# State sums by transposes, a gate by token and two value products in a fused sequence kernel

## The chip, the cores and the metric

The kernel runs on one core of a Trainium2 chip. The metric is the device time of one execution in microseconds (us). The engines are PE (TensorE: products and transposes; PEld is its weight load), DVE (VectorE), ACT (ScalarE), POOL (GpSimd) and SP (which issues most DMAs). Each works through its own queue in order.

## What is computed

Eight sequences of 256 tokens with 128 channels go through four double layers; everything is in float32, and after each part there is a residual sum and a layer norm. Two parts matter here. One is the local attention block (run twice, in two layers): 8 heads of 64, windows of 64 tokens, each token looks at its own window and the one before.

```python
bk, bv = (look_around(bk), look_around(bv))   # the window before, and the own one
sim = einsum('bhwid,bhwjd->bhwij', bq, bk)
mask = (i < j) | (i > j + WINDOW) | (j == -1)
attn = softmax(where(mask, -max, sim))
out = einsum('bhwij,bhwjd->bhwid', attn, bv)
```

The other is the Mamba block that follows, with 256 inner channels and 16 states:

```python
x_inner, z = split(x @ W_in)
xc = silu(conv(x_inner) + conv_b)
delta = softplus(delta_raw * w_dt + b_dt)      # delta_raw, B, C = xc @ W_xproj
h = exp(delta * A) * h + delta * B * xc        # a scan over the tokens, 16 states
y = sum over states of (h * C)
y = y + xc * D_param
return (y * silu(z)) @ W_out
```

The rest (a gated recurrence before; two mixtures of experts, two attention pairs and typed attention after) is not edited.

## The kernel before

The program is written in six stages: `rglru`, `local_mamba`, `moe1`, `chunked`, `moe2`, `typed`. In `local_mamba` the activations lie with the 128 channels on the partitions and the tokens along them. `one_sequence` (inside `local_mamba`, L1335) runs two local blocks and a norm for one sequence; four sequences are live at a time, and as each ends, `mamba_sequence` (L1223) for it is started beside the next ones (`interleave`, L256, called at L1470).

That is only the order in which instructions are recorded. `_Order` (L312) then sets the order on each engine: `plan` (L612) is a list scheduler with a cost table (`LENGTHS`, L352: how long each form keeps its engine, and when its result is there), a bias added to the priority of each engine, tile and stage (`BIAS`, L328), and a reluctance to change ACT's function table or the shape of PE's tiles (`STAY`, L327). The order that it finds is imposed on every engine's queue. It knows Exp and Ln as one group of functions.

The parts that the change touches:

- Values of the local block (L1124 to L1128). The attention of a 128-token half works on 64-token windows, so the values are needed for tokens 0 to 127, 64 to 191 and 128 to 255. For each of these three shifts one product `vps` of 128x512 is made on PE and copied from PSUM by ACT into `v[:, a, :]`. In the second half of the sequence the scores (L1142) take the keys `k[r, g, k0 : k0 + P]` with k0 = 64 for the queries 128 to 191, under the mask `band` that the tables hold (L148).
- The gate (L1246 to L1252): z with its channels on the partitions, Silu by ACT into `sz`. Two Silu and a load of the combined exponential and logarithm table (`exp_ln`, L898) follow each other there.
- Scan and state sums (L1293 to L1310). For each of 8 pairs of states: four exponentials `da` on ACT (L1302), and on DVE the product `hs` (L1304), the scan (L1306) and the product with C (L1307), each over 128x1024. Then PE adds the two states of the pair into one PSUM bank, `yp`, by a product with the identity matrix (L1309): two products of 128x512 per pair, 128 in the whole kernel. A float32 product is two instructions in the profile, so there are 256.
- The end (L1311 to L1317): DVE adds the skip term xc * D to the sum (L1313, two instructions per sequence, read from PSUM), POOL (DVE for the last sequence) multiplies with the gate (L1314), and the result goes as moving operand into the output projection `wout`.

L870 is the one line in `mm` that issues every product, so the profile tells these by their tiles.

Of the kernel before, what the change touches and what calls it, by code (L numbers as in the profile page):

```python
# [81 lines left out]
def _tables():  # L82
# [65 lines left out]
    madd("band", np.concatenate([mask((i < k0) | (i > k0 + 64)), mask((k0 < w) | (k0 > w + 64))], 1))  # L148
# [163 lines left out]
class _Order:  # L312
# [14 lines left out]
    STAY = dict(PE=80, ACT=740)  # L327
    BIAS = {  # L328
        "ACT  1": 100, "ACT  5": 585, "ACT bt 3": 5, "ACT bt 5": -775, "ACT d 2": -425, "ACT da 2": -45, "ACT e 2": -5, "ACT e 4": 965, "ACT e 6": -20,
        "ACT got 3": 575, "ACT h 2": -200, "ACT ix 4": 15, "ACT k 2": 265, "ACT lavp 2": 210, "ACT lnrs 1": -10, "ACT lnrs 2": -160, "ACT lnsq 1": -135,  # L330
        "ACT lnsq 2": 15, "ACT ot 2": 10, "ACT ptsb 2": -595, "ACT ptsb 6": -515, "ACT q 2": 20, "ACT qsq 2": 10, "ACT r 2": -5, "ACT rg 1": 10,
        "ACT rg 2": -915, "ACT rn 2": 15, "ACT rs 4": 340, "ACT rs 6": -690, "ACT s 6": 200, "ACT sakq 2": -10, "ACT sg 3": -550, "ACT sh 5": -2525,
        "ACT spe 1": -220, "ACT spt 1": -50, "ACT st 6": 100, "ACT sz 2": 280, "ACT v 2": 885, "ACT vs 4": 320, "ACT xchunked 2": 15, "ACT xs 2": -610,
        "DVE biasfull 3": -335, "DVE biaspart 3": -20, "DVE bt 5": -5, "DVE c 1": 590, "DVE centre 0": 320, "DVE d 2": 10, "DVE decaypart 4": -600,
        "DVE e 4": 570, "DVE four 4": 100, "DVE fs 4": -70, "DVE gate 4": 340, "DVE get 2": 200, "DVE got 4": 530, "DVE identb 0": -50, "DVE k 6": 500,
        "DVE lg 2": 2240, "DVE lo 4": -265, "DVE mv 4": -660, "DVE mv 5": 100, "DVE mv 6": -485, "DVE nm 2": -3975, "DVE nm 6": 4960, "DVE nth 4": -45,
        "DVE oh 2": -725, "DVE oh 5": -10, "DVE ptsb 2": -3895, "DVE ptsb 6": 895, "DVE put 4": -395, "DVE put 5": 55, "DVE q 5": -825, "DVE q 6": -475,
        "DVE rc 2": -1225, "DVE rc 6": 10, "DVE route 2": -55, "DVE s 5": 10, "DVE sares 2": 70, "DVE sel 2": -1590, "DVE sg 3": -140, "DVE sm 4": 2720,
        "DVE spl 1": -215, "DVE ss 2": 370, "DVE st 4": 85, "DVE st 6": 1645, "DVE sum 4": 170, "DVE t 2": 440, "DVE u 2": 250, "DVE vs 4": 50,
        "DVE we 4": 1425, "DVE xc 2": 460, "DVE xla 4": -15, "DVE xlocal 2": -5, "DVE xmoe 5": -200, "DVE xmoe 6": -580, "DVE xpf 4": -370,  # L340
        "DVE xrglru 2": 120, "DVE xsa 4": 80, "DVE z 4": -1990, "PE a 2": -100, "PE acc 5": 155, "PE b 2": -35, "PE bt 3": 75, "PE bt 5": 50,
        "PE cum 2": -995, "PE cum 4": -25, "PE cum 5": -615, "PE fold 2": 2915, "PE g 2": -4155, "PE gate 2": 785, "PE kps 4": 135, "PE less 2": 295,
        "PE lg 2": 1680, "PE lg 4": 50, "PE ln 2": -10, "PE o 2": 10, "PE o 6": -10, "PE pg 5": 150, "PE ps 4": -15, "PE pt 4": -130, "PE pu 3": 220,
        "PE py 3": -200, "PE py 5": 170, "PE qk 2": 25, "PE qkt 2": -720, "PE raw 2": -8675, "PE rows 2": 400, "PE sc 2": -50, "PE sc 4": 65, "PE sc 6": 5,
        "PE v 5": 290, "PE vps 2": 4075, "PE vps 4": 25, "PE wo 2": 75, "PE wo 6": -85, "PE wout 2": -115, "PE xin 2": 1180, "PE xps 2": -2540, "PE y 2": 20,
        "PE z 2": -450, "PE zt 5": 560, "PE zt 6": 25, "POOL d 2": 130, "POOL e 6": -30, "POOL got 4": -200, "POOL h 2": 370, "POOL k 5": 400,
        "POOL k 6": 850, "POOL km 6": 1240, "POOL mean 0": 1510, "POOL places 5": -200, "POOL q 6": 20, "POOL rest 4": -65, "POOL rg 1": -800,
        "POOL rg 2": -200, "POOL rot 2": -400, "POOL s 6": -750, "POOL t 2": 550, "POOL zero 0": -655, "POOL zeros 1": 385, "SP bc 2": -970, "SP cst 3": 5,
        "SP got 3": 355, "SP got 5": 350, "SP rottable 0": 80, "SP rows 4": 210, "SP rowschunked 4": -105, "SP vec 0": -830, "SP w 0": 15, "SP w 3": 115,
        "SP wattn 2": 585, "SP wffn 2": 705, "SP wlocal 0": 1175, "SP wmoe 4": 520, "SP xs 2": -105, "SP ybuf 5": -200,  # L350
    }
    LENGTHS = {  # L352
        "ACT  LoadActFuncSet  ": (1178, 1283), "ACT d Ln 128x512 128x512": (535, 640), "ACT da Exp 128x255 128x255": (398, 503),
        "ACT e Abs 128x256 128x256": (460, 565), "ACT e Exp 128x128 128x128": (420, 525), "ACT e Exp 128x256 128x256": (461, 566),
        "ACT e Exp 128x512 128x512": (527, 632), "ACT four Exp 128x2 128x2": (100, 205), "ACT got DMACopy 128x512 128x512": (454, 3611),
        "ACT h TensorCopy 64x255 64x255": (295, 400), "ACT lnrs Exp 128x256 128x256": (315, 420), "ACT ot TensorCopy 128x512 128x512": (486, 591),
        "ACT qsq Square 128x512 128x512": (494, 599), "ACT r Relu 128x256 128x256": (460, 565), "ACT rg Exp 128x1020 128x1020": (1039, 1144),
        "ACT rg Exp 128x1024 128x1024": (998, 1103), "ACT rg Ln 128x1024 128x1024": (950, 1055), "ACT rn Exp 128x16 128x16": (110, 215),
        "ACT rn Ln 128x16 128x16": (112, 217), "ACT rs Exp 128x2 128x2": (96, 201), "ACT rs Ln 128x2 128x2": (98, 203),
        "ACT sh Silu 128x512 128x512": (492, 597), "ACT v TensorCopy 128x512 128x512": (485, 590), "ACT xc Identity 128x256 128x256": (460, 565),  # L360
        "ACT xc Silu 128x512 128x512": (526, 631), "ACT xchunked TensorCopy 128x256 128x256": (263, 368), "ACT xmoe Identity 128x256 128x256": (404, 509),
        "ACT xs TensorCopy 33x256 33x256": (257, 362), "ACT xsq Square 128x128 128x128": (297, 402), "DVE biaspart TensorCopy 96x256 96x256": (197, 282),
        "DVE decay TensorScalarPtr 128x512 128x512": (508, 593), "DVE decaypart TensorCopy 128x512 128x512": (331, 416),
        "DVE four TensorScalarPtr 128x4 128x4": (76, 160), "DVE ge TensorScalarPtr 128x256 128x256": (380, 465),
        "DVE ge TensorScalarPtr 85x256 85x256": (372, 457), "DVE got TensorScalarPtr 128x128 128x128": (258, 343),
        "DVE h TensorTensor 128x256 128x256": (312, 397), "DVE hs TensorScalarPtr 128x1024 128x1024": (2189, 2274),
        "DVE hs TensorTensor 128x1024 128x1024": (1116, 1201), "DVE mv BNStatsAggregate 128x2 128x6": (82, 167),
# [404 lines left out]
class _Kernel:  # L772
# [450 lines left out]
    def mamba_sequence(self, b, x, y, na, das, work, scan):  # L1223
# [71 lines left out]
        for m in range(8):  # L1295
# [12 lines left out]
            for n in range(2):  # L1308
                self.mm(yp, self.ident, flat(hs[:, n]), m == 0 and n == 0, m == 7 and n == 1)  # L1309
# [1101 lines left out]
```

## Time and profile before

| | us |
|---|---|
| median of 3 runs | 1628.97 (1626.48 to 1629.37) |
| the profiled execution | 1644.68 |
| its span | 1642.9 |
| PE busy in the span | 1417.4 (86%) |
| DVE busy | 1102.3 (67%) |
| ACT busy | 968.6 (59%) |
| POOL busy | 587.5 (36%) |
| granted PE clock, mean | 0.942 |

The profile is one execution, some 15 us longer than the median of the runs. Shares over the whole span mix stages with different limits; the `local_mamba` stage lies between about 40 and 801 us and has to be read by itself. "Busy" of PE counts each instruction to its modelled end and so includes overlap with the next one; the distance between the starts of two instructions says how long one holds the queue. "Idle before, releaser" names the instruction whose end let the engine go on.

### The profile page before, as it was taken

Reading aid. Unit: us, or ns where it says so; the run is one execution under the profiler, and the core shown is the slowest. Engines: PE = TensorE matmul, PEld = TensorE weight load, DVE = VectorE, ACT = ScalarE, POOL = GpSimd, SP = SyncE. Lnnn points to the kernel's source line nnn. Section 1 sums busy time; section 2 is a strip of 40 time slices with the busy share of each in tenths; the row PEclk is TensorE's granted clock in tenths of the full one; section 3 lists DMA queues with packets and bytes.
Section 4 is the critical chain, followed back from the end, with each engine's and each line's share of the span. In section 5 each row is a group of like instructions: output and inputs, shape, how many; then the busy total and the mean of one; then the engine's idle time right before and its main releaser. Section 6 shows DMA issues by size and latency. Waiting matters only on the chain. (4 is left out here: it accounts for less than half of the span.)

```text
span 1642.9 us, 28581 instructions
## 1 busy us (share of the span) xinstructions
PE 1417.4 (86%) x10826; PEld 909.4 (55%) x10826; DVE 1102.3 (67%) x2182; ACT 968.6 (59%) x2656; POOL 587.5 (36%) x535
## 2 busy tenths in 40 slices
PE   2688998989898887777579999999998899899997
PEld 1354554545554544334366766777675576556664
DVE  5745568898989898698545557554546333279886
ACT  3777888787978869446125545455453222167775
POOL 1334544535462523101431222212212102467774
PEclk7789999989999999779789999999998899999998
DMA  5000012121212223155430000000000130000000
GB/s 199 1 1 1 1 40 65 40 60 45 65 40 65 53 52 91 52 179 189 151 119 1 8 12 11 10 5 8 32 18 24 46 121 26 26 9 8 5 8 11
DMA packets 45113, 77.97 MB, mean 47 GB/s; under 512 B 5580, under 2 KB 21988, under 8 KB 43824
## 3 DMA queue, kind: packets, MB, share of 16 engines
q1 hardware_dynamic: 39648, 70.02, 14.0%
q0 software_dynamic: 3216, 5.07, 1.1%
q8 instruction: 85, 1.39, 0.4%
q10 hardware_dynamic: 2112, 1.05, 0.2%
q14 instruction: 52, 0.43, 0.1%
HBM read 66.87 MB, written 10.76 MB: 47 GB/s over the span
## 5 line engine op out<-in xcount | busy, mean ns | idle before, releaser
L870 PE MATMUL y<-hs,ident 128*128 128x512 f32 x256 | 139.7, 659 | 35.9 <-DVE hs L1307 35.6
L1158 POOL TENSOR_TENSOR e<-e,rc 128x1024 f32<-128x1024 f32 x32 | 78.0, 2437 | 202.7 <-DVE rc L1157 194.3
L1306 DVE TENSOR_TENSOR_SCAN hs<-da,hs 128x1024 f32<-128x1024 f32 x64 | 149.1, 2331 | 0.2
L2259 ACT ACTIVATE e<-sc,nm 128x128 f32<-128x128 f32 (+1 forms) x256 | 105.2, 427 | 46.6 <-DVE nm L2254 40.3
L1153 ACT ACTIVATE e<-sc,nm,rn 128x128 f32<-128x128 f32 x256 | 114.3, 466 | 13.8 <-DVE nm L1148 13.5
L981 PE MATMUL pt<-ident,e 128*128 128x128 f32 x768 | 114.2, 278 | 9.4 <-POOL e L1158 4.9
L1302 ACT ACTIVATE da<-d,na 128x255 f32<-128x255 f32 x256 | 109.3, 504 | 17.5 <-DVE hs L1306 13.7
L1836 POOL TENSOR_TENSOR e<-e,rc 128x512 f32<-128x512 f32 x32 | 34.0, 1064 | 219.8 <-DVE rc L1835 154.2
L981 PEld LDWEIGHTS pt<-ident,e 128*128 128x128 f32 x768 | 88.5, 141 | 42.5 <-issue 16.1
L2262 POOL TENSOR_TENSOR e<-e,rc 128x1024 f32<-128x1024 f32 x48 | 90.8, 1896 | 39.1 <-DVE rc L2261 32.1
L1105 POOL TENSOR_TENSOR t<-t,t 128x512 f32<-128x512 f32 x64 | 83.9, 1316 | 58.0 <-DVE t L1092 51.6
L1811 ACT COPY kp<-kps 128x512 f32<-128x512 f32 x128 | 74.7, 583 | 49.0 <-PE kps L870 46.4
L1658 POOL DMA_INDIRECT got<-ybuf,get x48 | 45.7, 952 | 159.2 <-DMA ybuf<-ys 97.1
L870 PEld LDWEIGHTS y<-hs,ident 128*128 128x128 f32 x256 | 48.5, 205 | 82.5 <-DVE hs L1307 54.2
L1304 DVE TENSOR_TENSOR hs<-u,bc 128x1024 f32<-128x1024 f32 x64 | 84.3, 1328 | 2.9 <-POOL u L1291 2.9
L1307 DVE TENSOR_TENSOR hs<-hs,bc 128x1024 f32<-128x1024 f32 x64 | 80.6, 1260 | 0.0
L1847 ACT COPY vs<-vps 128x512 f32<-128x512 f32 x64 | 37.4, 585 | 67.1 <-PE vps L870 53.6
L983 DVE COPY ptsb<-pt 128x512 f32<-128x512 f32 x104 | 68.8, 675 | 11.6 <-PE pt L981 9.3
L870 PE MATMUL qk<-w_local,h 128*128 128x512 f32 x128 | 69.3, 631 | 7.5 <-DVE t L1092 7.1
L870 PE MATMUL vps<-sa_vp,x_lf 128*32 128x512 f32 x512 | 68.4, 594 | 0.0
L1847 DVE COPY vs<-vps 128x512 f32<-128x512 f32 x64 | 43.3, 682 | 37.2 <-PE vps L870 25.1
L2057 DVE TENSOR_TENSOR sh<-sh,pu 128x512 f32<-128x512 f32 x32 | 22.0, 688 | 67.1 <-PE pu L870 54.0
(380 smaller groups left out, 3782.4 us busy)
## 6 DMA issues: line engine op xcount, KB each, us to landing
bc<-xs SPq DMA_DIRECT2D x128, 256.0 KB
w_moe<-in_e_dram SPq DMA_DIRECT2D x16, 768.0 KB
w_attn<-in_w_dram SPq DMA_DIRECT2D x4, 1024.0 KB
w_local<-in_w_dram SPq DMA_DIRECT2D x2, 1557.0 KB
places<-zeros SPq DMA_DIRECT2D x2, 1280.0 KB
got<-places SPq DMA_DIRECT2D x6, 256.0 KB
ybuf<-ys SPq DMA_DIRECT2D x8, 160.0 KB
x_in<-in_x_dram SPq DMA_DIRECT2D x1, 1024.0 KB
```

The lines of the kernel that those rows point to most:

```text
L870: return self.nc.tensor.matmul(out, lhsT, rhs, start=start, stop=stop)
L981: self.last = self.nc.tensor.transpose(pt[:, j * P : (j + 1) * P], src[:, j * P : (j + 1) * P], self.ident)
L1105: nc.gpsimd.tensor_add(t1, t1, t2)
L1153: nc.scalar.activation(e[:, j, g, :], scs[:, j, g, :], AF.Exp, bias=nm[:, j, g : g + 1], scale=rq[:, j, g : g + 1], accum_out=sm[:, j, g : ...
L1158: nc.gpsimd.tensor_tensor(e, e, rc.unsqueeze(3).to_broadcast([P, 2, 4, P]), ALU.mult)
L1302: nc.scalar.activation(da[:, n, c, 1:S], d[:, c, 1:S], AF.Exp, scale=na[:, i : i + 1])
L1304: nc.vector.tensor_tensor(hs, u.unsqueeze(1).to_broadcast(shp), bn, ALU.mult)
L1306: nc.vector.tensor_tensor_scan(line(hs), line(da), line(hs), 0.0, ALU.mult, ALU.add)
L1307: nc.vector.tensor_tensor(hs, hs, cn, ALU.mult)
L1847: i = copy(v[:, c, :, :].rearrange("p a b -> p (a b)"), ps)
L2259: nc.scalar.activation(e[:, i, :], sc[:, i, :], AF.Exp, bias=nm[:, i : i + 1], accum_out=sm[:, i : i + 1])
L2262: nc.gpsimd.tensor_tensor(e, e, rc.unsqueeze(2).to_broadcast([P, n, keys]), ALU.mult)
```

## The change

Five things are done, all in `local_mamba`; the planner's numbers are new as well.

1. Values: two products, tokens 0 to 127 and 128 to 255, each copied by ACT as before. The middle window is put together by DVE from the same two PSUM banks: partitions 64 to 127 of the first and 0 to 63 of the second, each where they lie. So the middle window holds its two halves exchanged; the keys are read with their halves exchanged (a reversed access pattern), and the mask's rows likewise.
2. State sums: instead of a product with the identity, PE transposes each 128x128 block of `hs` (four per state) and lets the transposes add up in the same PSUM bank. The sum then has the tokens on the partitions.
3. Skip term: ACT scales xc by D in place, after `u` has been made of it, and four more transposes add it to the sum.
4. Gate by token: z is made with tokens on the partitions (x as the stationary operand, the weights moving, the same number and width of products). One DVE product of 128x512 multiplies the sum in PSUM with `sz`.
5. Back: four transposes per sequence bring the gated sum to channels on partitions again, ACT copies it from PSUM, and `wout` follows.

```diff
+    late = mask((k0 < w) | (k0 > w + 64))
+    late[:64] = np.roll(late[:64], 64, 1)
+    madd("band", np.concatenate([mask((i < k0) | (i > k0 + 64)), late], 1))
...
-    STAY = dict(PE=80, ACT=740)
+    STAY = dict(PE=190, ACT=1060)
...
+        "DVE v TensorCopy 64x512 64x512": (197, 282),
+        "PE y Matmult 128x128 128x128": (130, 300), "PE yg Matmult 128x128 128x128": (136, 312),
...
-        for a in range(3):
+        for t in range(2):
             ps = self.psum("Q", "vps")
-            self.mm(ps, h[:, 64 * a : 64 * a + P], w[:, l, 1024:1536])
-            nc.scalar.copy(v[:, a, :], ps)
+            self.mm(ps, h[:, t * P : (t + 1) * P], w[:, l, 1024:1536])
+            half = slice(64 - 64 * t, P - 64 * t)
+            nc.scalar.copy(v[:, 2 * t, :], ps)
+            nc.vector.tensor_copy(v[half, 1, :], ps[half, :])
...
+                        keys = k[r, g, k0 : k0 + P]
+                        if k0 == 64:
+                            keys = keys.rearrange("p (a b) -> p a b", a=2)[:, ::-1, :]
...
-            for c in range(2):
-                self.mm(ps[:, c * S : (c + 1) * S], win[:, 256 + c * P : 256 + (c + 1) * P], x)
+            for t in range(2):
+                self.mm(ps[:, t * S : (t + 1) * S], x[:, t * P : (t + 1) * P], win[:, 256:512])
...
+            [nc.scalar.mul(xc[:, c, :], xc[:, c, :], self.v("dpar", c)) for c in range(2)]
         yield 3.0
-        yp = self.psum("Y", "y")
+        yp = self.psum("Y", "y").rearrange("p (t c d) -> p t c d", t=2, c=2)
+
+        def gathered(src, first, last):
+            for c in range(2):
+                for t in range(2):
+                    self.nc.tensor.matmul(
+                        yp[:, t, c, :], src[:, c, t * P : (t + 1) * P], self.ident, start=first and c + t == 0, stop=last and c + t == 2, is_transpose=True
+                    )
...
-                self.mm(yp, self.ident, flat(hs[:, n]), m == 0 and n == 0, m == 7 and n == 1)
+                gathered(hs[:, n], m == 0 and n == 0, False)
             yield 2.3
-        yg = tile("t")
+        gathered(xc, False, True)
+        nc.vector.tensor_tensor(flat(sz), yp.rearrange("p t c d -> p (t c d)"), flat(sz), ALU.mult)
+        ps = self.psum("M", "yg")
         for c in range(2):
-            nc.vector.scalar_tensor_tensor(yg[:, c, :], xc[:, c, :], self.v("dpar", c), yp[:, c * S : (c + 1) * S], ALU.mult, ALU.add)
-        eng.tensor_mul(yg, yg, sz)
+            for t in range(2):
+                nc.tensor.transpose(ps[:, c * S + t * P : c * S + (t + 1) * P], sz[:, t, c * P : (c + 1) * P], self.ident)
+        nc.scalar.copy(flat(sz), ps)
         ps = self.psum("M", "wout")[:, 0:S]
         for c in range(2):
-            self.mm(ps, wout[:, c, :], yg[:, c, :], c == 0, c == 1)
+            self.mm(ps, wout[:, c, :], sz[:, c, :], c == 0, c == 1)
```

Besides these lines the planner's table of biases is replaced: 175 entries before, 188 after, no value kept, in all stages; most lengths move by under 3%. So the order of instructions differs in every stage, also where no line of the computation does.

## The prediction

> **What bounds the kernel now.** The chain that ended last reaches back only into the last stage (from 1581 us on), so it says nothing of the part that changes. The busy digits of the 40 slices show that part, the local and Mamba blocks, between about 40 and 801 us, with PE, DVE and ACT all high. So I cut it into three stretches: before the first scan, the steady part in which one Mamba sequence runs beside local blocks, and the drain. The view is the busy time by stretch; its columns are the stretch, its length, busy us (and instructions) of PE, PEld, DVE, ACT, POOL, then the granted PE clock, DMA share and GB/s.
>
> ```profile
> 40.00:252.00 212.00, 175.26 (x1131) 105.99 (x1129) 129.09 (x220) 165.51 (x441) 93.87 (x108) 0.93 0.03 9
> 252.00:640.00 388.00, 339.48 (x1933) 202.03 (x1934) 346.16 (x427) 314.88 (x822) 173.37 (x145) 0.97 0.21 56
> 640.00:801.00 161.00, 114.12 (x497) 61.49 (x496) 129.56 (x143) 83.17 (x186) 36.25 (x24) 0.86 0.45 148
> ```
>
> In the first stretch PE (83%) and ACT (78%) carry the load and DVE has room. In the steady part DVE is busiest: 346.2 of 388 us, 89%; PE has 339.5 (87.5%), ACT 314.9 (81%). In the drain DVE leads by far. So the change takes work from the second engine of the steady part, not the first. What remains for PE to give is DVE's idle time. By the view of who waited for whom, DVE sat idle 41 us in the steady part, 15.5 of it ended by PE and 25 by ACT; in the drain 14 ended by PE and 13 by ACT. The largest of its waits from 252 to 801 us (columns: us in total, times, longest):
>
> ```profile
> DVE t L1284 <- ACT e L1282: 13.9, 5, 3.4
> DVE x_mamba L925 <- ACT ln_rs L924: 11.0, 4, 3.8
> DVE s L1319 <- PE wout L870: 10.2, 3, 5.7
> DVE nm L1147 <- PE sc L870: 5.0, 6, 2.3
> ```
>
> The two longest are for ACT, and the third is the output projection, whose own chain the change lengthens. ACT in turn idled 43 us for PE in the steady part, so part of what DVE waits for at ACT is PE's.
>
> The groups of instructions that the change touches, or that carry the load (busy us, mean ns of one | idle before):
>
> ```profile
> L1306 DVE TENSOR_TENSOR_SCAN hs<-da,hs 128x1024 f32<-128x1024 f32 x64 | 149.1, 2331 | 0.2
> L870 PE MATMUL y<-hs,ident 128*128 128x512 f32 x256 | 139.7, 659 | 35.9 <-DVE hs L1307 35.6
> L1128 ACT COPY v<-vps 128x512 f32<-128x512 f32 x48 | 28.0, 594 | 12.9 <-PE vps L870 12.7
> L1313 DVE SCALAR_TENSOR_TENSOR t<-xc,vec,y 128x256 f32<-128x256 f32 x16 | 7.3, 473 | 0.5 <-PE y L870 0.5
> ```
>
> The state sums idle PE for DVE: the scans are late, not the sums. A mean of 659 ns is a latency; the cost in PE's queue is the distance between starts, from the timeline (start, us, what):
>
> ```profile
> 433.19 0.60 PE L981 MATMUL pt<-ident,e 128*128 128x128 f32 x4
> 433.63 1.02 PE L870 MATMUL vps<-w_local,h 128*128 128x512 f32 x2
> 434.49 1.02 PE L870 MATMUL y<-hs,ident 128*128 128x512 f32 x2
> 435.35 0.59 PE L870 MATMUL g<-h,w_local 128*85 128x256 f32 x2
> ```
>
> Four transposes hold PE 0.44 us (433.19 to 433.63); a product of 512 columns is two instructions and holds it 0.86 us, for vps as for y.
>
> **The change, part by part.**
>
> *PE.* State sums: 128 products become 512 transposes, 128 x (0.86 - 0.44) = -53.8 us. Values: 48 products become 32, 16 x 0.86 = -13.8. Added: per sequence four transposes of the skip term and four of the gated sum, 8 x 2 x 0.44 = +7.0. The z products keep their number and width, 0. Sum -60.6 us, of which (by where y and vps lie now) about -5 in the first stretch, -38 in the steady part, -17 in the drain. The unknown: the trace has fp32 transposes, none that adds into PSUM. If adding costs nothing it is 0.44 us for four; if it makes two passes of each, as the products have, it is 0.86 and the -53.8 is gone. I take 0.44, since among the products adding costs nothing: y adds and vps does not, and both hold 0.86 us. Weight loads: each transpose loads its own block, 141 ns by the transposes' rows against 205 ns, two per sum; they overlap and already keep 0.109 us spacing, so 0.
>
> *DVE.* Added: 32 copies of 64x512 from PSUM for the middle window. No such row exists. These are the nearest:
>
> ```profile
> L1713 DVE COPY ys<-py 80x512 f32<-80x512 f32 x8 | 5.5, 687 | 3.9 <-PE py L870 3.9
> L2220 DVE COPY vm<-v 128x128 f32<-128x128 f32 x16 | 4.6, 285 | 1.9 <-PE v L870 1.9
> ```
>
> The time goes with the columns, not the partitions (80 partitions take 687 ns), so 0.68 us, 22 us in all; the low end is 0.285 (9 us), which is also what the new table of lengths in the diff writes for it. Removed: 16 of L1313, -7.6; added: 8 products with the gate from PSUM at 0.69, less the one of L1314 that DVE did for the last sequence, +4.8. In the steady part (10 layers' copies, 5 sequences) that is 13 - 4.7 + 3.5 = +12 us, or +4 at the low end: DVE goes from 346 to 358 (or 350) us. In the drain -1.4. POOL loses 7 gate products of 1.27 us; its wait there was for DVE, so 0.
>
> *ACT.* Minus 16 v copies x 0.59 = -9.4; plus 8 copies of the transposed gate x 0.59 = +4.7; plus 16 scalings of the skip term, bounded by the 64x255 copy (0.40) and the two-operand Identity (0.57), taken as the da exponential with one operand (0.50) = +8. And a hidden one: with the new biases the order of the changed program has 83 table loads instead of 69, all of the surplus in this stage, because exponentials and logarithms now slip in between a Gelu or Silu and the combined set's load. A load costs this (ACT timeline):
>
> ```profile
> 259.18 1.30 ACT L1302 ACTIVATE da<-d,na 128x255 f32<-128x255 f32 x3
> 260.50 1.28 ACT L1201 ACT_TABLE_LOAD   x1
> 261.80 1.20 ACT L1201 ACTIVATE ge<-g,vec 128x256 f32<-128x256 f32 x3
> ```
>
> From the end of the work before to the start after it is 1.31 us: 14 x 1.31 = +18.3. ACT's sum is +21.6: -5 in the first stretch, +15 in the steady part (315 to 330 us, 85%), the rest in the drain. The Trainium skill, "ScalarE: Activation LUTs", section "What ACT_TABLE_LOAD costs", adds a drain of about 1.38 us to each switch; by it the surplus would be 14 x 2.66 = 37 us. This trace shows no such gap, so the rows decide.
>
> The scaling of the skip term must wait until u has read xc (POOL, 1.27 us). In the changed order it stands behind scan exponentials that wait for the same d, so I cost the wait at 0; uncovered it would be 1.27 us x 7 = 9 us of ACT, with the next exponentials behind it.
>
> *The gate chain* of a sequence, from its last state product: now the sum 0.86, two L1313 0.87, gate 0.69 (1.27 on POOL). After: transposes 0.44 + 0.44, gate 0.69, four transposes 0.44, ACT copy 0.59. 2.4 against 2.6 us, plus one more hand-over: even.
>
> *Order elsewhere.* The biases move the later stages too; their instructions and table loads are the same in number. From 860 to 1258 us PE is busy 391 of 398 us, where order has nothing to give. The last stage (1400 to 1643, PE 92%) is most reordered: I take 0, with 6 us either way.
>
> **The sum.** First stretch: PE -5, ACT -5, both on the path: -4. Steady part: DVE has +12 of work; of its 41 us idle I let go 10 of the 15.5 ended by PE, and 8 of the 25 ended by ACT, because ACT waits less for PE but has 15 us more to do: -18 + 12 = -6. Drain: -1.4 of DVE and a little of the 14 ended by PE, most of it the output chain that stays: -3. Together -13 us of the profiled execution's 1644.7 (span 1642.9), so 1631.7. The runs' median is 1629.0; the same 13 us off it give 1616.
>
> **Rivals.**
>
> *PE sets the pace, and its saving comes through.* For it: PE is 87.5% busy and ACT idles 43 us for it. Against: PE itself waits for hs. DVE's PE-ended idle in steady part and drain goes (-30), half of the ACT-ended goes (-13), the first stretch gives 8, DVE's extra work takes 11 back: -40, 1589 us.
>
> *Nothing to measure*: what DVE gains in idle it pays in copies; 1629, within 0.2% (3.3 us, about what runs of this kernel can tell from no change).
>
> *Slower: ACT takes PE's place as DVE's late supplier.* Place: the steady part. ACT at 85% with more table loads keeps DVE's idle share at today's 10.8%; then 358 us of DVE need 358/0.892 = 402 us, +14; less 3 elsewhere, +11: 1640 us. It decides once more than about 37 of DVE's 41 idle us stay. For it: DVE's two longest waits are for ACT. Against: the copies may cost 0.285.
>
> *The change doesn't do what it says*: transposes that add take two passes; PE keeps 0.86 per sum and ACT and DVE pay all the same: about +15, 1644.
>
> **How the numbers follow.** Chances: forecast 0.50, PE's saving 0.18, nothing 0.12, ACT's lateness 0.17, two passes 0.03. Faster 0.68, same 0.12, slower 0.20. The range takes in both unknown costs (copies at 0.285: -8 more; the last stage +-6) and the first and third rivals' centres: 1589 to 1640.
>
> **What would show it.** Right: starts of y transposes 0.109 us apart; PE in the steady part down to some 78% busy while DVE rises above 91%; 83 table loads. The copies' row decides 0.68 or 0.285. Wrong: DVE idle in the steady part near 41 us with ACT its releaser (slower), or below 10 (much faster); y spacing 0.216; or a last stage that moved by over 6 us. A clock well under the 0.97 of the steady part would show that PE's freed time is paid back in slower instructions (at 0.77, in the stretch from 60 to 105 us, PE is only 67% busy); I count nothing for it, as PE then has room.

## The result, and the profile after

The changed kernel takes 1653.9 us (median of 4 runs, 1653.4 to 1654.4) where the kernel before takes 1628.2 on the same chip: a ratio of 1.0155 [1.0141, 1.0168], 25.7 us slower. The profiled execution takes 1653.7 us, span 1651.6. Chips differ by about one per cent (the kernel before takes 1628 us on one, 1643 to 1646 on those of its profile and of the experiments), so every ratio below is within one chip. Profiles are compared by the end of the edit's stage and by the last stage, not by their totals, since what lies between, with the same work, took 624 us in the profile of after and 638 to 643 in all others named here.

Busy time by stretch of the changed kernel; columns as before, the last two stretches being the one bound by PE and the last stage:

```profile
40.00:252.00 212.00, 171.49 (x1152) 106.61 (x1150) 141.59 (x237) 166.72 (x446) 98.47 (x111) 0.93 0.03 9
252.00:640.00 388.00, 313.75 (x2075) 211.58 (x2074) 342.32 (x429) 322.15 (x804) 162.93 (x137) 0.92 0.21 56
640.00:801.00 161.00, 96.37 (x596) 71.57 (x594) 136.02 (x138) 94.86 (x217) 20.85 (x14) 0.80 0.45 145
860.00:1258.00 398.00, 396.18 (x4547) 277.42 (x4548) 228.63 (x708) 201.40 (x466) 87.68 (x97) 0.99 0.04 12
1400.00:1651.00 251.00, 236.08 (x1871) 137.86 (x1869) 177.62 (x420) 143.84 (x620) 152.28 (x104) 0.98 0.03 10
```

PE did get its time back: 339 to 314 us in the steady part, 114 to 96 in the drain. But DVE is no busier than before in the same 388 us: 342, so it still idles 46 us there (before: 42). The granted clock has fallen, 0.97 to 0.92 and 0.86 to 0.80. The groups that answer to those of before (line, engine, tiles, shapes, count | busy us, mean ns | idle before):

```profile
L1302 PE MATMUL y<-ident,hs 128*128 128x128 f32 x512 | 87.0, 313 | 52.6 <-DVE hs L1319 52.4
```

```profile
L1318 DVE TENSOR_TENSOR_SCAN hs<-da,hs 128x1024 f32<-128x1024 f32 x64 | 150.2, 2358 | 0.1
L1128 DVE COPY v<-vps 64x512 f32<-64x512 f32 x32 | 21.9, 684 | 9.8 <-ACT v L1127 9.1
L1324 DVE TENSOR_TENSOR sz<-y,sz 128x512 f32<-128x512 f32 x8 | 5.4, 678 | 2.7 <-PE y L1302 2.7
```

The state sums lost 53 us of PE's busy time, and PE idles 17 us longer in front of them, for the same scans. The copies take 684 ns each, not the 282 of the table of lengths, and DVE stood another 10 us in front of them, 9 of it until ACT's eviction of the same PSUM tile had ended. Four of DVE's longest waits from 252 to 801 us (us in total, times, longest):

```profile
DVE t L1287 <- ACT e L1285: 17.4, 6, 5.8
DVE ss L1084 <- ACT qsq L1083: 9.5, 8, 2.5
DVE nm L1150 <- PE sc L868: 9.4, 7, 2.5
DVE s L1334 <- PE wout L868: 7.3, 4, 3.8
```

ACT is still what it waits for most. Two numbers cut the loss in two. The last sequence's logits leave PSUM (the end of the stage that the edit touches) at 812.8 us, before at 800.7: +12. From 40 us to that end DVE is busy 623.2 us (before 604.5) and idle 149.5 us (before 156.2): 18.7 us more work, and only 6.7 us less idle time. And the last stage, whose code is untouched, takes 214.6 us from its first product with `km` to the end, before 200.8: +14. Together 26, the whole loss.

### The profile page after: what moved, and what is told of

It reads as the page before. It is cut to its first block, busy times and chain, and to the rows that moved or that the text cites. A ratio compares the mean times of both kernels' runs of the same rounds, so it can differ in the third digit from the quotient of the medians.

```text
span 1651.6 us, 29190 instructions
## 1 busy us (share of the span) xinstructions
PE 1385.2 (84%) x11114; PEld 928.5 (56%) x11114; DVE 1125.0 (68%) x2205; ACT 992.5 (60%) x2678; POOL 575.0 (35%) x528
## 3 DMA queue, kind: packets, MB, share of 16 engines
q10 hardware_dynamic: 2112, 1.05, 0.2%
## 4 chain that ended last, share of the span: by engine, by line
PE 57%; DVE 20%; ACT 13%; issue 6%; POOL 3%; DMA 1%; ACTq 0%; SPq 0%; DVEq 0%; POOLq 0%
PE sc L868 8%; PE vps L868 8%; PE kps L868 7%; PE out L868 4%; PE pt L979 4%; DVE hs L1318 4%; PE pu L868 3%; PE pg L868 3%; PE o L868 3%; ACT e L1156 2%; DVE hs L1316 2%; DVE hs L1319 2%; ACT da L1314 2%; PE py L868 2%; PE hps L868 2%
## 5 line engine op out<-in xcount | busy, mean ns | idle before, releaser
L1302 PE MATMUL y<-ident,hs 128*128 128x128 f32 x512 | 87.0, 313 | 52.6 <-DVE hs L1319 52.4
L979 PE MATMUL pt<-ident,e 128*128 128x128 f32 x768 | 118.4, 282 | 15.2 <-POOL e L1161 9.1
L1156 ACT ACTIVATE e<-sc,nm,rn 128x128 f32<-128x128 f32 x256 | 114.7, 465 | 19.2 <-DVE nm L1151 18.7
L1302 PEld LDWEIGHTS y<-ident,hs 128*128 128x128 f32 x512 | 69.1, 162 | 73.8 <-DVE hs L1319 66.0
L868 PE MATMUL qk<-w_local,h 128*128 128x512 f32 x128 | 69.8, 637 | 15.5 <-DVE v L1128 7.8
L981 ACT COPY ptsb<-pt 128x512 f32<-128x512 f32 x88 | 51.5, 586 | 33.5 <-PE pt L979 32.8
L2269 DVE TENSOR_REDUCE nm<-sc 128x4 f32<-128x1024 f32 (+1 forms) x48 | 58.6, 1220 | 15.4 <-PE sc L868 15.3
```

What stands on the lines that cost most here:

```text
L868: return self.nc.tensor.matmul(out, lhsT, rhs, start=start, stop=stop)
L979: self.last = self.nc.tensor.transpose(pt[:, j * P : (j + 1) * P], src[:, j * P : (j + 1) * P], self.ident)
L981: copy(sb.rearrange("p a b -> p (a b)"), pt)
L1156: nc.scalar.activation(e[:, j, g, :], scs[:, j, g, :], AF.Exp, bias=nm[:, j, g : g + 1], scale=rq[:, j, g : g + 1], accum_out=sm[:, j, g : ...
L1302: self.nc.tensor.matmul(yp[:, t, c, :], src[:, c, t * P : (t + 1) * P], self.ident, start=first and c + t == 0, stop=last and c + t == 2, ...
```

## The experiments

The expectations of the first eight name three theories: *edit* (the changed instructions cost the time), *plan* (the new biases and STAY, and the order that they write, cost it), and *unfitted plan* (biases found for one program cost by themselves when another is planned with them). "Stage ends" is the start of the copy of the last sequence's logits, "last stage" the time from the first `sc<-km` product to the end, both from the profile.

| | kernel | ratio to before, 95% | stage ends | last stage |
|---|---|---|---|---|
| | before, first profile | 1 | 800.7 | 200.8 |
| | after | 1.0155 [1.0141, 1.0168] | 812.8 | 214.6 |
| e1 | before once more | one run, 1646.1 us | 802.3 | 200.8 |
| e2 | edit, old biases | 1.0243 [1.0223, 1.0264] | 848.2 | 200.8 |
| e3 | old code, new biases | 1.0277 [1.0255, 1.0299] | 835.7 | 214.8 |
| e4 | edit, new biases in its stage only | 1.0201 [1.0170, 1.0232] | 831.8 | 200.8 |
| e5 | after once more | 1.0174 [1.0144, 1.0205] | 805.8 | 214.6 |
| e6 | whole edit, before's order | 1.0109 [1.0079, 1.0139] | 821.1 | 201.0 |
| e7 | values alone, before's order | 1.0086 [1.0059, 1.0113] | 813.4 | 200.9 |
| e8 | sums alone, before's order | 1.0076 [1.0051, 1.0101] | 813.1 | 201.0 |
| e9 | after, last stage in before's order | 1.0052 [1.0029, 1.0074] | 807.3 | 202.6 |
| e10 | e8, sums by products | 1.0066 [1.0043, 1.0089] | 812.8 | 201.0 |
| e11 | e7, copies on GpSimd | 1.0011 [0.9993, 1.0028] | 802.3 | 200.8 |
| e12 | e8, last sequence as before | 1.0055 [1.0035, 1.0075] | 809.7 | 202.5 |
| e13 | e8, skip scaled by GpSimd | 1.0108 [1.0086, 1.0130] | 819.5 | 200.8 |
| e14 | e9, copies on GpSimd | 1.0039 [1.0024, 1.0055] | 811.3 | 200.8 |
| e15 | e14, skip scaled by GpSimd | 1.0145 [1.0126, 1.0163] | 830.0 | 202.6 |
| e16 | e8, no scaling | 1.0064 [1.0040, 1.0088] | 811.7 | 201.0 |
| e17 | e8, not turned back | 1.0005 [0.9990, 1.0019] | 800.7 | 201.0 |
| e18 | e8, neither | 0.9975 [0.9959, 0.9991] | 800.0 | 201.0 |

### Edit or plan: e1 to e5

e1 and e5 are the two kernels unchanged. e2 has the changed code with before's STAY, its 175 biases and its lengths, e3 before's code with after's, e4 the changed code with after's STAY and the biases whose keys end in " 2" (the stage of the edit), and before's for all others. The lines of STAY in e2, and of e4:

```diff
-    STAY = dict(PE=190, ACT=1060)
+    STAY = dict(PE=80, ACT=740)
```

```diff
-    STAY = dict(PE=190, ACT=1060)
+    STAY = {2: dict(PE=190, ACT=1060), 0: dict(PE=80, ACT=740)}
...
-                        far = self.STAY.get(e, 0) if g is not None and state[e][0] is not None and g != state[e][0] else 0
+                        far = self.STAY[2 if self.stage[item[1]] == 2 else 0].get(e, 0) if g is not None and state[e][0] is not None and g != state[e][0] else 0
```

> The kernel before, unchanged, for a second profile of it: the one shown took 1644.7 us, 16 us more than the median of its runs (1628.2), so a comparison with it hides 16 us of the 25. If both theories below are to be told apart by stage, this profile must be near 1628 us. Theory 'edit' expects the 16 us to have been lost in the local and Mamba stage of the first profile (so that this stage ends near 785 us here, not 801); theory 'plan' expects them in the later stages, whose instructions are the same in both kernels (the last stage near 230 us instead of 243).

> The changed kernel with the old biases, old table and tile reluctances and old lengths (only the three new forms' lengths added). Theory 'edit' (the extra 22 us on DVE and the extra work on ACT cost the time, whatever the order): slower than before by 15 to 25 us, about 1645 to 1653. Theory 'plan' (the new order costs it): within 8 us of before, 1620 to 1636. A third, 'unfitted plan' (numbers searched for one program fit no other): slower than the changed kernel itself, over 1655.

> The computation before under the new biases, reluctances and lengths. Theory 'edit': near before, 1625 to 1637. Theory 'plan': slower by 15 to 25 us, 1643 to 1653, with the last stage some 10 us longer than in the kernel before. 'Unfitted plan': slower by over 10 us too, but in the local and Mamba stage.

> The changed kernel with the new biases and reluctances in the local and Mamba stage alone, and the old ones (and old lengths) in every other stage. If the last stages' new order is what costs, 10 to 15 us less than the changed kernel, 1639 to 1644 ('plan'). If the loss lies in the local and Mamba stage, no less than 5 us of the changed kernel's 1654: 1649 or more ('edit').

> The changed kernel, unchanged, beside the experiments on one chip, with a profile. The earlier pair of profiles came from chips on which the kernel before takes 1628 and 1645 us. Both theories: ratio to before 1.012 to 1.018. By stage, against the second profile of before: theory 'plan' expects the last stage 12 to 16 us longer and the local and Mamba stage up to 12; theory 'edit' expects 20 us and more in the local and Mamba stage.

Every mixture of the two is slower than either kernel whole, e3 most, though e4's interval overlaps that of e5: each set of biases suits the program that it came with. So these three can't say what the edit costs; a theory that sets the edit against the plan has to hold the order still. What they do say is in the last column: the last stage takes 214.6 to 214.8 us in every kernel planned there with the new numbers, even with the old code, and 200.8 to 202.6 in every other. e5's runs spread (1661 to 1673 us; its profile is of the fastest), but its last stage is that of after to a tenth.

### The order held still: e6 to e8

The planner's order is replaced by before's, written out. Each instruction stands where it stood, a changed one in the place of the one that it replaces, an added one as soon as its operands are there; all have before's 69 table loads. e6 is the whole edit, e7 the values part alone, e8 the sums, gate and skip part alone.

```diff
     def impose(self):
-        order, _ = self.plan()
+        order = json.loads(zlib.decompress(base64.b85decode(self.KEPT)))
```

> The whole edit of the computation in the order of the kernel before: every instruction that both programs have stands where it stood, a transpose group takes its product's place, and the new instructions follow their inputs. 69 table loads as before. Theory 'plan' (the re-searched order costs the 25 us): 0.990 to 1.003 of before. Theory 'edit' (22 us of DVE copies and the ACT work cost it in any order): 1.008 to 1.016.

> The value edit alone (two products, middle window copied by DVE), in the order of the kernel before. PE loses 13.8 us, ACT 9.4, DVE gains 21.9. 'Edit': the copies come through on the busiest engine, 1.005 to 1.012 of before. 'Plan': 0.998 to 1.005.

> The transposes that add up, the gate by token and the skip term on ACT alone, three value products as before, in the order of the kernel before. PE loses 47 us, DVE 3, ACT gains 13. 'Edit' (DVE and ACT set the pace, PE does not): 0.997 to 1.005. 'Plan': 0.985 to 0.998.

Both parts cost, each by itself 0.8%, with no bias and no table load changed. The values part adds 22 us of copies to DVE and is 14 us slower; what share is the copies' own, e11 tells. The sums part gave PE 47 us back (53.8 less 7.0, by the spacing of the starts) and is slower all the same. The two costs, 14 and 13 us, don't add up: the whole edit is 18 us slower. In the old order it ends its stage 19 us late, in its own order 3.5 (e5 against e1) to 12 (after against the first profile of before): the new biases do help the stage that they were made for.

### Four single reasons: e9 to e12

e9: after with before's biases (the keys that end in " 6") and STAY in the last stage only; the instructions there are in before's order, all others in after's.

```diff
+    STAY_TYPED = dict(PE=80, ACT=740)
...
-                        far = self.STAY.get(e, 0) if g is not None and state[e][0] is not None and g != state[e][0] else 0
+                        far = (self.STAY_TYPED if self.stage[item[1]] == 6 else self.STAY).get(e, 0) if g is not None and state[e][0] is not None and g != state[e][0] else 0
```

> The whole changed kernel, with its new biases and STAY everywhere but in the last stage (the one that begins with the products of the ternary weights and ends with the output), where the biases and the STAY of before choose the order; its instructions there stand in exactly the order of before, and in all other stages exactly in the order of after. ORDER theory: the last stage's 14 us are the new biases' own, so it falls from 214.7 to 200.8 us and the ratio from 1.016 or 1.017 (two measurements of after) to 1.007 to 1.009. CARRIED-OVER theory (the last stage is longer for something that the earlier stages leave behind, such as late tiles or transfers): it stays near 214 us and the ratio at 1.016 or more.

The order theory holds: 1.0155 and 1.0174 become 1.0052. Why this order costs is seen in the last stage's busy times, PE's first: after, then e9, then before once more (e1). The number of PE's instructions is the same.

```profile
1436.90:1651.60 214.70, 199.78 (x1698) 114.30 (x1698) 164.44 (x396) 134.80 (x606) 133.56 (x86) 0.98 0.02 7
```

```profile
1447.80:1650.50 202.70, 187.02 (x1698) 112.63 (x1698) 161.91 (x395) 133.83 (x606) 133.27 (x86) 0.96 0.03 8
```

```profile
1443.40:1644.30 200.90, 185.12 (x1698) 111.90 (x1698) 161.56 (x395) 133.92 (x606) 133.21 (x86) 0.98 0.03 8
```

PE does not wait longer, it works longer. The products of this stage come in three tile sizes (64 rows for `km`, 32 columns for `o`, 128x128 for the rest). The new order changes size 221 times, before's 179. From start to start a product of 64 rows or 32 columns after its own kind takes 0.007 us in the median, a 128x128 block 0.109, but one after a change 0.203, or 0.31 from 64 rows to 128.

More than half of the loss is one pattern. Two products with `km` that follow each other start 0.007 us apart and run side by side: four instructions in 1.06 us. In after 14 such products stand alone, in e9 and e1 none, and one alone takes 1.05 us, no less than two together. Before once more (e1), then after (start, us, what):

```profile
1464.30 1.13 PE L870 MATMUL sc<-km,q 64*128 64x512 f32 x4
```

```profile
1514.59 1.12 PE L868 MATMUL sc<-km,q 64*128 64x512 f32 x2
1515.64 0.44 PE L959 MATMUL zt<-ident,s 128*128 128x128 f32 x2
1516.01 1.12 PE L868 MATMUL sc<-km,q 64*128 64x512 f32 x2
```

Seven pairs taken apart are 14 x 1.05 - 7 x 1.06 = 7.3 us. By stretches of one tile size, each from its first start to the start of the next, those of 64 rows are 9.3 us longer than in e1 (65.3 against 56.0), those of 128x128 3.8 us and those of 32 columns 0.4; what the pairs don't explain goes with the other changes of size. The products with `km` in e9 and then after have the same count and mean, and less overlap:

```profile
L1040 PE MATMUL sc<-km,q 64*128 64x512 f32 x192 | 54.7, 647 | 0.8 <-DVE mv L1119 0.8
```

```profile
L868 PE MATMUL sc<-km,q 64*128 64x512 f32 x192 | 64.0, 640 | 0.8 <-DVE s L2078 0.8
```

The Trainium skill, "TensorEngine Tiling (Array Packing)", section "Key Properties", says that a change of tiling mode drains TensorE. It gives no price; the distances between starts above do.

e10: e8 with PE's price returned, and nothing else.

```diff
-                        yp[:, t, c, :], src[:, c, t * P : (t + 1) * P], self.ident, start=first and c + t == 0, stop=last and c + t == 2, is_transpose=True
+                        yp[:, t, c, :], src[:, c, t * P : (t + 1) * P], self.ident, start=first and c + t == 0, stop=last and c + t == 2
```

> The kernel with the sums' part alone in the order of before (1.0076 of before), its 512 transposes of the state sums and the 32 of the skip term issued as ordinary products with the identity: same operands, same output, same order, same token layout and the same gate chain; only TensorE's price returns, some 0.9 us for four in place of 0.44, about 59 us more of it in all. WORTHLESS theory (TensorE's freed time lies beside the chain of VectorE and is partly paid back by a lower granted clock): ratio stays between 1.005 and 1.012, and the clock of 640 to 802 us comes back from 0.76 to about 0.85. WORTHWHILE theory (the transposes do shorten the stage, and the token layout's chain takes more than that back): 10 us or more on top, ratio 1.014 or above.

The worthless theory, to the letter. Steady part and drain of e8, and of e10:

```profile
252.00:640.00 388.00, 314.93 (x2122) 212.88 (x2122) 338.26 (x416) 313.25 (x816) 166.29 (x141) 0.96 0.22 56
640.00:802.00 162.00, 105.20 (x608) 78.04 (x608) 135.81 (x141) 94.19 (x214) 30.02 (x19) 0.76 0.50 147
```

```profile
252.00:640.00 388.00, 344.62 (x2462) 251.49 (x2462) 337.00 (x415) 312.49 (x813) 165.66 (x141) 0.97 0.21 56
640.00:802.00 162.00, 117.37 (x792) 97.48 (x793) 136.32 (x139) 94.85 (x216) 29.25 (x18) 0.84 0.50 142
```

With PE 30 us busier in the steady part, DVE does the same work in the same time. In the drain part of the loss is paid by the clock, which is 0.84 again. Over the whole stage, from 40 us to its end, PE is busy 644.3 us in e10 and 603.0 in e8, and DVE idle 169.1 and 169.8. So the transposes, right as they are, save nothing in this place.

e11: e7 with the copies made by GpSimd, from SBUF, out of what ACT has just evicted.

```diff
-            nc.vector.tensor_copy(v[half, 1, :], ps[half, :])
+            nc.gpsimd.tensor_copy(v[half, 1, :], v[half, 2 * t, :])
```

> The values edit alone in the order of before (1.0086 of before), with its 32 copies taken from VectorE: GpSimd copies the 64x512 halves in SBUF, out of what ScalarE has just evicted. COPIES theory (the 22 us of copies on VectorE were the whole cost of the edit): VectorE is back at before's busy time, products and evictions stay one third fewer (PE -14, ACT -9 us), ratio 1.000 or a little under, at most 1.003. LATENESS theory (what costs is that the middle third of the values comes later, whichever engine brings it): GpSimd's copy is no sooner there than VectorE's, ratio stays at 1.006 or above.

The copies theory: 12 of 14 us are back. The run takes away the copies' time on DVE, DVE's wait in front of them and the longer hold of the PSUM tile together. GpSimd's copy takes 1.05 us in the mean (0.61 in the median, up to 2.57), but GpSimd has the room (193 of 388 us busy in the steady part):

```profile
L1643 POOL COPY v<-v 64x512 f32<-64x512 f32 x32 | 33.4, 1045 | 31.8 <-ACT v L1642 26.0 <-ACT rn L1612 4.8
```

DVE is not quite back at before's work: from 40 us to the end of the stage it is busy 610.0 us (e1: 604.5), the same instructions taking longer, the 32 small products `nm<-nm,rn` 12.2 us in place of 9.4. What is left is level with before: a third fewer value products and evictions (PE -14, ACT -9 us) bring nothing that these runs can tell from no change.

e12: e8, but the last sequence (b = 7) takes its sums as before, and z, skip term, gate and output product likewise.

```diff
-                gathered(hs[:, n], m == 0 and n == 0, False)
+                if b < B - 1:
+                    gathered(hs[:, n], m == 0 and n == 0, False)
+                else:
+                    self.mm(yflat, self.ident, flat(hs[:, n]), m == 0 and n == 0, m == 7 and n == 1)
```

> The sums' part alone in the order of before (1.0076 of before), but the last of the eight sequences computes its sums, skip term and gate as before does. END theory (the longer chain behind the last scan is a third of the cost of 11 us: 17.4 us to the last logits' copy in place of 13.2): the chain is 13.2 us again and the ratio 1.004 to 1.006. MIDDLE theory (the cost arises before: sequences 4 to 6 come late by more and the end only passes it on): chain 13 us, but ratio 1.006 to 1.008. CLOCK theory (the drain is longer since the granted clock falls to 0.76 where TensorE idles): the clock of 640 to 802 us rises with the last sequence's products to 0.8 or more and the ratio falls below 1.004.

Between end and middle, and not to be told from e8 by the ratio (the intervals overlap). The chain from the start of the last scan to the logits' copy is 14.5 us, not 17.4, at a clock of 0.79 in the drain; most of the cost was already there before it.

### What the sums part pays for: e13 to e18

e13 is e8 with the skip term scaled by GpSimd; e14 is e9 with e11's copies; e15 is e14 with e13's scalings. e14 and e15 have e9's order.

```diff
-            [nc.scalar.mul(xc[:, c, :], xc[:, c, :], self.v("dpar", c)) for c in range(2)]
+            [nc.gpsimd.tensor_scalar_mul(xc[:, c, :], xc[:, c, :], self.v("dpar", c)) for c in range(2)]
```

> The sums' part alone in the order of before (1.0076 of before), with the 16 scalings of the skip term (128x256, about 0.45 us each on ScalarE) on GpSimd. SCALING theory (they stand ahead of ScalarE's squares and evictions, which VectorE waits for): VectorE's wait on the squares falls back from 10.1 to about 5 us between 252 and 640 us, the seven us of sequences 1 to 7 go, and the ratio is 1.002 to 1.004. CHAIN theory (the cost is the gate chain behind the last scan of each sequence): wait and ratio stay, 1.006 to 1.009.

> The changed kernel with the last stage in the order of before (1.0052 of before), every instruction where that kernel has it, but the 32 copies of the values moved from VectorE to GpSimd, out of SBUF. COPIES theory: as in the old order, where this took 12 us back (1.0086 to 1.0011), the stage up to the logits ends 8 to 12 us sooner and the ratio is 0.998 to 1.000. ORDER theory (the new order was fitted with the copies in it, and its cost lies elsewhere): less than 4 us come back, ratio 1.003 or more.

> As the kernel with the copies on GpSimd in the changed kernel's order, and the 16 scalings of the skip term on GpSimd too. SCALING theory: another 4 to 7 us come back, ratio 0.993 to 0.997, a version that beats both kernels. CHAIN theory: no difference to the kernel before it by more than 2 us.

e13 and e15 can't tell what the scalings cost on ACT: GpSimd needs 2.0 us for one (2.4 in e15). From 252 to 640 us DVE's wait for the squares falls from 10.1 us in e8 to 7.3 in e13, but a new one takes its place, `h` for ACT's `ln_rs`, which rises from 2.4 to 14.5.

```profile
L1813 POOL TENSOR_SCALAR xc<-xc,vec 128x256 f32<-128x256 f32 x16 | 31.8, 1992 | 49.5 <-DVE lg L1866 49.2
```

e14 is a miss: in the new order, moving the copies takes the ratio from 1.0052 to 1.0039, two us with overlapping intervals, where in the old order it returned 12; in its profile the stage even ends 4 us later than in e9's. From 40 us to that end DVE's busy time falls by 11.1 us only (623.0 to 611.9), not by the 21.9 of the copies, since other instructions take longer, as in e11 (`nm<-nm,rn` 12.9 us in place of 8.8), and its idle time rises by 15.1 us. Why it idles more stays open.

e16 to e18 are e8 with work left out: the scaling; the turn of the gated sums back to channels; both. The first line goes in e16 and e18, the others in e17 and e18.

```diff
-            [nc.scalar.mul(xc[:, c, :], xc[:, c, :], self.v("dpar", c)) for c in range(2)]
...
-        ps = self.psum("M", "yg")
-        for c in range(2):
-            for t in range(2):
-                nc.tensor.transpose(ps[:, c * S + t * P : c * S + (t + 1) * P], sz[:, t, c * P : (c + 1) * P], self.ident)
-        nc.scalar.copy(flat(sz), ps)
```

> The sums' part alone in the order of before (1.0076 of before); the 16 scalings of the skip term are left out, so the skip term goes in unscaled. SCALING theory: ScalarE's 7 us were what made VectorE wait for its squares and the Mamba front; ratio 1.002 to 1.004 and the wait on the squares between 252 and 640 us back near 5 us. CHAIN theory: 1.006 to 1.008.

> The sums' part alone in the order of before (1.0076 of before); the gated sums are not turned back to channels (the 32 transposes, their 8 PSUM tiles and 8 evictions are left out), so the output product takes them in the token layout. CHAIN theory: the turn is what lengthens the way from a sequence's last scan to its logits and holds a PSUM buffer of the shared ring; the end chain is 15 us or less in place of 17.4, ratio 1.002 to 1.004. SCALING theory: the end chain is shorter by 2 to 3 us, and nothing else: 1.006 or so.

> The sums' part alone in the order of before, with both left out: no scaling of the skip term and no turn back to channels; what is left of the edit is the transposes that add up in PSUM, z by tokens, and a product with the gate out of PSUM in place of three operations. If the two additions are the whole cost, 0.997 to 1.001; if the layout or the order costs by itself, 1.003 or above.

The turn is the cost: without it 1.0076 becomes 1.0005, and the stage ends at 800.7 us instead of 813.1. It is little work, eight times four transposes and an eviction. From 40 us to that end DVE is busy 603.3 us in both kernels, so the whole difference is idle time of DVE: 169.8 us in e8, 157.5 in e17 (157.8 in e1). Its waits for the output product, the scores and the squares, from 40 us to the end of the stage, in before once more (e1), e8 and e17:

```profile
DVE s L1319 <- PE wout L870: 10.2, 3, 5.7
DVE nm L1147 <- PE sc L870: 20.7, 15, 4.0
DVE ss L1086 <- ACT qsq L1085: 18.8, 22, 2.7
```

```profile
DVE s L1850 <- PE wout L1389: 16.3, 4, 5.4
DVE nm L1666 <- PE sc L1389: 22.9, 17, 4.0
DVE ss L1605 <- ACT qsq L1604: 23.6, 27, 2.7
```

```profile
DVE s L1844 <- PE wout L1388: 6.5, 2, 4.0
DVE nm L1665 <- PE sc L1388: 20.3, 17, 4.0
DVE ss L1604 <- ACT qsq L1603: 21.6, 25, 2.7
```

Most of it is the wait for the output product, 9.8 us less without the turn (7.6 if 2.2 us without a releaser in front of the same instruction of e17 are counted). It lies in the last four sequences: from the end of a sequence's last product with C to the start of its residual sum these four take 35.0 us in e8, 27.0 in e17 and 31.0 in e1. In the first four DVE does not wait there at all. The scores and squares give 4.6 us more. For these the way can lead over ACT, whose instructions start in the order in which they are written. ACT's eviction in e8 (from 40 to 815 us):

```profile
L1845 ACT COPY sz<-yg 128x512 f32<-128x512 f32 x8 | 4.7, 585 | 9.7 <-PE yg L1844 6.1 <-issue 3.6
```

Twice its own time ACT stands before it, until the transposes have come. 5.7 us of this lie in the first five sequences, where squares that DVE waits for are among the next instructions of ACT; that these are late for this reason fits the order and is not shown by a run of its own. The scaling costs 2 us by e16 against e8 (within the intervals) and 5 by e18 against e17 (at their edge). With both left out the kernel is 0.25% faster than before, about 4 us: no more than that are PE's 47 us worth here, and 1 us of it can be DVE's (busy 603.5 us, in e1 604.5).

The end of the last sequence shows the two losses together. PE in e8 (start, us, what [idle before]):

```profile
782.41 1.97 PE L1818 MATMUL y<-ident,hs 128*128 128x128 f32 x8
786.97 1.10 PE L1818 MATMUL y<-ident,hs 128*128 128x128 f32 x8 [1.30 <-DVE hs L1835]
791.43 1.85 PE L1818 MATMUL y<-ident,hs 128*128 128x128 f32 x8 [3.36 <-DVE hs L1835]
795.88 1.97 PE L1818 MATMUL y<-ident,hs 128*128 128x128 f32 x8 [2.60 <-DVE hs L1835]
```

Eight transposes take 1.10 us at 786.97, and after an idle time of 3.36 us 1.85 and 1.97; at 782.41 they took 1.97 as well. The idle times of 3.36 and 2.60 us are 2.47 and 1.20 in front of the same sums in e1, which take longer. Then the way from the gate to the residual sum, in e8 and in before once more (e1):

```profile
802.25 0.69 DVE L1840 TENSOR_TENSOR sz<-y,sz 128x512 f32<-128x512 f32 x1 [0.56 <-issue]
803.00 1.12 PE L1844 MATMUL yg<-ident,sz 128*128 128x128 f32 x4 [0.78 <-issue]
804.15 0.58 ACT L1845 COPY sz<-yg 128x512 f32<-128x512 f32 x1 [3.60 <-issue]
804.79 2.07 PE L1389 MATMUL wout<-sz,w 128*128 128x256 f32 x4 [0.67 <-ACT sz L1845]
806.90 0.42 DVE L1850 TENSOR_TENSOR s<-wout,x_local 128x256 f32<-128x256 f32 x1 [3.96 <-PE wout L1389]
```

```profile
795.82 0.69 DVE L1314 TENSOR_TENSOR t<-t,sz 128x512 f32<-128x512 f32 x1
796.56 1.13 PE L870 MATMUL wout<-t,w 128*128 128x256 f32 x4 [1.88 <-DVE t L1314]
797.73 0.42 DVE L1319 TENSOR_TENSOR s<-wout,x_local 128x256 f32<-128x256 f32 x1 [1.22 <-issue]
```

From gate to residual 4.65 us against 1.91: 1.8 for the turn, 0.9 because four products of `wout` take 2.07 us in place of 1.13. Behind it lie the norm and the logits: 6.2 us to the logits' copy in place of 4.6.

No version here that computes the whole beats the kernel before; the nearest is the values part with the copies on GpSimd, level with it.

## Why the prediction was wrong

It said 1616 us and got 1653.9, 38 us off: 25 in the stage of the edit (13 faster foretold, 12 slower measured) and 14 in the last.

- **"The last stage ... I take 0, with 6 us either way": failed**, +14 us. The reason given, that instructions and table loads are the same in number, counts PE's instructions and not what each one follows. The order there sets whether the products with `km` run in pairs (7.3 us) and how often the tile size changes (221 times, not 179). e9 takes the loss away with nothing but order, and e3 makes it with none of the edit.
- **"2.4 against 2.6 us, plus one more hand-over: even": failed.** In before's order the turn costs 12 us (e8 against e17). Counted from the last product with C to the residual sum, the chain is no even trade: 35.0 us in the last four sequences with the turn, 27.0 without it, 31.0 in before. There DVE waits for its end. In the changed kernel's own order no run takes the turn out.
- **"of its 41 us idle I let go 10 of the 15.5 ended by PE, and 8 of the 25 ended by ACT": failed.** In the steady part nothing went (46 us, before 42). DVE's added work was right, +18.7 us in the stage where the terms give 22 - 7.6 + 4.8 = 19.2, so the forecast of -13 needed some 32 us of its idle time to go; 6.7 went (15.0 in e5 against e1). PE's load does not make that idle time: with 41 us more of it the idle time is the same (e8, e10).
- **"First stretch ... -4": came, but not for its reason.** The first scan starts at 245.2 us, in before at 252.7; in before's order the same edit has it at 257.1 (e6; e1: 254.4), so it is the new order and not the work taken from PE and ACT.
- **The copies: right** in duration (0.68, 22 us), against the planner's 282 ns, and in sign. In before's order they are the cost of the values part, 12 of its 14 us (e7, e11); the products and evictions saved there bring nothing that can be told from no change.
- **PE's saving: right as an amount** (transposes that add start 0.109 us apart, like those that don't), and worth 0 to 4 us (e10, e18). The two-pass rival is out.
- **ACT's 14 more table loads: right as a count** (83), and not what decides. Kernels with 69 loads are slower than before too (e6 to e8), and e9, in after's order up to the last stage and with 83, is faster than e6. What the 14 cost by themselves no run shows.
- **"I count nothing for" the clock: wrong in a small way.** It fell as feared, and PE does need its speed where the last chain has nothing beside it: at most 2.5 us at the end (0.9 at `wout` and 1.6 behind it, e8 against e1).
- **The slower rival had the right place**: DVE's idle stayed and ACT was its main releaser, 25.9 us of some 44. Its price (1640) lacks the last stage.

Open: why DVE idles more with the copies on GpSimd in the one order and not in the other; whether the part of the turn's cost that is not the wait for the output product comes by ACT's standing or by the PSUM tile that the turn holds in a shared ring (e17 takes both away); and how much of after's own 3 to 12 us in its stage (two profiles) is copies, turn or clock, since only the old order took them apart.

## What to carry to other kernels

Time taken from an engine that is second in line is worth nothing until a wait is found that its load, and not its latency, makes: give the load back in one experiment and see whether the wait changes. A short operation added to a chain is priced by how much later the engine at its end can start, hand-overs included, not by its own length. And a planner's numbers are part of the change in every stage that they order, so a stage with untouched code is to be measured like the others.

## What the runs showed of the hardware that was not expected

- PE pays for a change of tile size, 0.20 us from start to start (0.31 from 64 rows to 128) where the same kind follows itself in 0.007 to 0.109, and more for a pair taken apart: two products of 64 rows take 1.06 us side by side and 1.05 each alone. An order with 42 more changes, seven pairs among them taken apart, made the last stage 14 us longer with the same instructions.
- With less work PE's clock was lower in e8's drain, 0.76, where e10, which gives the sums back as products, has 0.84. Whether the shorter time or the kind of instruction makes it, e10 does not separate. Less work alone is not enough: e8's steady part has 0.96 with 315 us of PE, after's 0.92 with 314. The Trainium skill, "TensorE: Matmul & The Clock Gate", section "What's actually happening", names an idle window of about 3.4 us, after which the clock is half. The trace agrees only in part: eight transposes take 1.85 us in place of 1.10 behind an idle time of 3.36 us, but also 1.97 at 782.41, with no idle time over 2.15 us in the 17 us before.
- Copies on GpSimd made other instructions of DVE longer: 5.5 us in all in e11, where DVE has the same work as in e1.
- GpSimd took 2.0 us (0.9 to 3.6) to scale 128x256 by a column, where its product of two 128x512 takes 1.27 and ACT scales the same in 0.50.
